# A 2-D convolution block on one NeuronCore: the copy of a rotated half moves from ScalarE to GpSimd

## The chip, the core and the metric

The kernel runs on one NeuronCore of one Trainium2 chip. Five engines work side by side: TensorE (PE, matmuls; its weight loads are PEld), VectorE (DVE), ScalarE (ACT), GpSimd (POOL) and SyncE (SP, which here only issues DMAs). The metric is the device time of one execution in microseconds (us). Before the change it was 19,064.78 us, the median of three runs from 19,036.86 to 19,088.58.

## The reference

The input is x, 4 images of 512 x 512 places with 16 channels, in float32. Two layers follow each other, each with a group normalisation in front and a residual sum behind:

```python
# --- layer 0 (conv_preact) ---
x = x + _L0_conv_ref(_gn(x), L0_conv_h0, L0_conv_numerators, L0_conv_denumerator)
# --- layer 1 (conv_preact) ---
x = x + _L1_conv_ref(_gn(x), L1_conv_kernel, L1_conv_bias, L1_conv_radius)
```

Layer 0 is a convolution by a rational filter, carried out in the frequency domain. Its core is

```python
X = jnp.fft.rfft2(x, s=(2 * l1, 2 * l2), axes=(-3, -2))
Y = jnp.einsum('...hwi,ijhw->...hwj', X, H_full)
y = jnp.fft.irfft2(Y, s=(2 * l1, 2 * l2), axes=(-3, -2))
return y[..., :l1, :l2, :]
```

so at each of the frequencies, 16 input channels are mixed into 16 output channels by a matrix of complex numbers. Layer 1 is a 3 x 3 convolution normalised by the norms of its input and kernel, with an arccosine behind it.

## The kernel before

The program is written in Python with a framework that tracks the tiles, inserts all semaphores, and fills each engine's queue itself: an instruction can stand in its engine's queue earlier than its place in the program, when the framework's own planning finds it ready. Each engine works through its queue in order, so an instruction that waits holds everything behind it.

Four phases run one after the other. `filter_phase` builds the filter, `forward_phase` transforms x along the width, `conv_phase` does the rest of layer 0's convolution, and `last_phase` transforms back and computes layer 1. The change lies in `conv_phase` alone.

`conv_phase` (from L650) works row by row, a row being one frequency along the width. There are 513 of them (L673). The convolution along the height is cut into blocks: for each row there are an overlapped transform of x in 128 frequencies f, 16 input channels with their complex parts on 128 partitions, and a matrix gh of the filter. The tile `xe` of a row (L727) holds 8 "places" of 1,024 numbers a partition:

- place 0 is the transform of the row itself, written by `x_part` (L723) from TensorE's result px;
- places 1 to 3 and 5 to 7 are shifted by 16, 32, ... partitions. They are made through HBM: `x_late` (L738) stores place 0 into `xf_d` with GpSimd's DMA (`store(0, ...)`, L745), multiplies it on GpSimd by a rotation (four multiplies L752, one multiply L753, one add L754, giving the tile `xl`), and stores `xl` too (`store(1, ...)`). `load_xe` (L766) then loads the six places in two DMAs of 1,536 KB (L769), issued by SP;
- place 4 is shifted by 64 partitions: its lower half is the upper half of place 0, its upper half the lower half of `xl`. `half_shift` (L760) copies each half on ScalarE (L763), 64 partitions x 1,024 numbers.

`mix` (L792) multiplies all 8 places by gh into the PSUM tile pm; this is the einsum. `g_part` (L775) makes the next row's gh from g; `over_q` (L812) and `over_g` (L842) take the result back along the height and store it into y_d (L868).

The rows overlap, as written out by hand in `step(n)` (L876): it mixes row n, makes gh of row n + 1, begins x of row n + 2 (`x_part` and `x_late` behind the first quarter, k = 0; `half_shift` behind the third and fourth, k = 2 and 3), and finishes rows n - 1 and n - 2. Loads run ahead: x of row n + 3, g of row n + 2, and the shifted places of row n + 1. Evictions from PSUM (`evict`, L678) go two to ScalarE, one to VectorE in turn. `xl` has one buffer, `xe` three, g and x two each; PSUM has three buffers for pg, two for pm and three shared by px, pz and py.

The queues of a row in the trace, around the change: ACT's is xe (from px), the copy of the plain half, yf, turn, gh, zq, the copy of the rotated half, yf, gh, zq, yo, yf, gh, zq. POOL's is two multiplies L752, the store of place 0, two more, L753, L754, the store of xl, the store of y_d, and the two operations of over_q, zd (L836) and z (L838). SP's is the first xe load, g, the second xe load, x.

Of the kernel before, what the change touches and what calls it, by code (L numbers as in the profile page):

```python
# [46 lines left out]
P = 128  # L47
# [153 lines left out]
def bc(ap, axis, shape):  # L201
    return ap.unsqueeze(axis).to_broadcast(shape)
# [447 lines left out]
def conv_phase(tc, cst, g_d, x_d, y_d):  # L650
    nc = tc.nc
    with ExitStack() as ctx:
# [22 lines left out]
        state = {}  # L675
# [9 lines left out]
        def load_g(n):  # L685
            rc, r, plane = rows[n]
            g = io.tile([P, C, 8 * C], F32, name="g")
            t, w = g.rearrange("p j x -> p (j x)"), C * 8 * C
            if plane is None:
                nc.sync.dma_start(out=t, in_=dram(g_d[rc], r, 0, [w, P], [1, w]))  # L690
            else:
                for to, at in ((0, (0, 96)[plane]), (64, (64, 32)[plane])):
                    nc.sync.dma_start(out=t[to : to + 32], in_=dram(g_d[rc], r, at * w, [w, 32], [1, w]))
                    nc.gpsimd.memset(t[to + 32 : to + 64], 0.0)
            state["g", n] = g

        def load_x(n):
            rc, r, plane = rows[n]
            x = io.tile([P, B, 8 * C], F32, name="x")
            t, w = x.rearrange("p b x -> p (b x)"), B * 8 * C  # L700
            if plane is None:
                nc.sync.dma_start(out=t, in_=dram(x_d[rc], r, 0, [w, P], [1, w]))
            else:
                nc.gpsimd.memset(t[S:], 0.0)
                nc.sync.dma_start(out=t[:S], in_=dram(x_d[rc], r, plane * S * w, [w, S], [1, w]))
            state["x", n] = x

        def turn_x(n):

            for k in range(2) if n == 0 else [n // 64 + 1] if n % 64 == 0 else []:  # L710
                if k < 9:
                    state["own", k] = xlp.tile([P, 2, 64], F32, name="own", bufs=3)
                    nc.sync.dma_start(
                        out=state["own", k].rearrange("p v n -> p (v n)"), in_=cst["own"][:, 128 * k : 128 * k + 128]
                    )
            own, at = state["own", n // 64], slice(n % 64, n % 64 + 1)
            t = xlp.tile([P, 2 * F], F32, name="turn")
            nc.scalar.activation(t, dfs[:, 1], AF.Identity, scale=own[:, 1, at])
            m = xlp.tile([P, 2 * F], F32, name="dfs_n", bufs=2)
            nc.vector.scalar_tensor_tensor(m, dfs[:, 0], own[:, 0, at], t, ALU.mult, ALU.add)  # L720
            state["dfs", n] = m

        def x_part(n, b):  # L723

            if b == 0:

                state["xe", n] = xep.tile([P, 8, F, 2, 2, 2], F32, name="xe")  # L727
            if b % 2 == 0:
                state["px"] = ps_f.tile([P, 2, F, 2], F32, name="px", tag="full")
            px = state["px"]  # L730
            nc.tensor.matmul(px[:, b % 2].rearrange("p f c -> p (f c)"), state["x", n][:, b],
                             state["dfs", n], start=True, stop=True)
            if b % 2:
                evict(state["xe", n][:, 0, :, b // 2], px.rearrange("p k f c -> p f c k"))
            if b == B - 1:
                del state["x", n], state["dfs", n]

        def x_late(n):  # L738

            xe = state["xe", n][:, 0]  # L740
            fl = xe.rearrange("p f h c k -> p f (h c k)")

            def store(half, t):
                at = slice(C, P) if half == 0 else slice(0, P - C)
                nc.gpsimd.dma_start(out=xf_d[n % 4][half * P :, :][at], in_=t[at].rearrange("p f x -> p (f x)"))  # L745

            store(0, fl)
            xl = xlp.tile([P, F, 2, 2, 2], F32, name="xl")
            u = xlp.tile([P, F, 2, 2, 2], F32, name="xu")
            for c in range(2):  # L750
                for h in range(2):
                    nc.gpsimd.tensor_mul(u[:, :, h, c], xe[:, :, h, 1 - c], bc(late[:, 1 + c], 2, [P, F, 2]))  # L752
            nc.gpsimd.tensor_mul(xl.rearrange("p f h c k -> p f (h c k)"), fl, bc(late[:, 0], 2, [P, F, 8]))  # L753
            nc.gpsimd.tensor_add(xl.rearrange("p f h c k -> p (f h c k)"),  # L754
                                 xl.rearrange("p f h c k -> p (f h c k)"),
                                 u.rearrange("p f h c k -> p (f h c k)"))
            store(1, xl.rearrange("p f h c k -> p f (h c k)"))
            state["xl"] = xl

        def half_shift(n, half):  # L760

            dst, src = ((slice(0, 64), state["xe", n][64:, 0]), (slice(64, P), state["xl"][:64]))[half]
            nc.scalar.copy(state["xe", n][dst, 4].rearrange("p f h c k -> p (f h c k)"),  # L763
                           src.rearrange("p f h c k -> p (f h c k)"))

        def load_xe(n):  # L766
            src = xf_d[n % 4]
            for t in (1, 5):
                nc.sync.dma_start(  # L769
                    out=state["xe", n][:, t : t + 3].rearrange("p t f h c k -> p t (f h c k)"),  # L770
                    in_=bass.AP(tensor=src.tensor, offset=src.offset + t * C * XF,
                                ap=[[XF, P], [C * XF, 3], [1, XF]]),
                )

        def g_part(n, j):  # L775


            if j % 4 == 0:
                state["pg"] = [ps_g.tile([P, 4, F], F32, name=f"pg{c}", tag="pg") for c in range(2)]
            g, pg = state["g", n], state["pg"]  # L780
            for c in range(2):
                half = slice(64 * c, 64 * c + 64)
                nc.tensor.matmul(pg[c][:, j % 4], g[half, j], dg[half], start=True, stop=True)  # L783
            if j == 3:
                state["gh", n] = ghp.tile([P, F, 2, C], F32, name="gh")
            if j % 4 == 3:
                for c in range(2):
                    evict(state["gh", n][:, :, c, j - 3 : j + 1], pg[c].rearrange("p j f -> p f j"))
            if j == C - 1:
                del state["g", n]  # L790

        def mix(n, g):  # L792

            if g % 8 == 0:
                state["pm"] = ps_m.tile([P, 8, 8, 2 * B], F32, name="pm")
            xe, gh, pm = state["xe", n], state["gh", n], state["pm"]
            for q in range(4):
                f = g + 32 * q
                nc.tensor.matmul(  # L799
                    pm[32 * q : 32 * q + 32, g % 8], gh[:, f].rearrange("p c j -> p (c j)"),  # L800
                    xe[:, :, f].rearrange("p t h c k -> p t (h c k)"), start=True, stop=True,
                )
            if g == 7:

                state["y", n] = yp.tile([P, 16, 32, 4], F32, name="yf")
            if g % 8 == 7:
                evict(state["y", n][:, :, g - 7 : g + 1].rearrange("p t g x -> p g t x"),
                      pm.rearrange("p g t (h x) -> p g (t h) x", h=2))
            if g == 31:
                del state["xe", n], state["gh", n]  # L810
# [65 lines left out]
        def step(n):  # L876


            def row(k):
                return 0 <= n + k < n_rows  # L880

            if row(3):
                load_x(n + 3)
            if row(2):
                load_g(n + 2)
            if row(1):
                load_xe(n + 1)
            for k in range(4):
                if row(0):
                    for g in range(8):  # L890
                        mix(n, 8 * k + g)
                if row(1):
                    for j in range(4):
                        g_part(n + 1, 4 * k + j)
                if row(-1):
                    for t in range(4):
                        over_q(n - 1, 4 * k + t)
                if row(2) and k == 0:
                    for m in range(B):
                        x_part(n + 2, m)  # L900
                    x_late(n + 2)
                if row(2) and k >= 2:
                    half_shift(n + 2, k - 2)
                if row(3) and k == 2:
                    turn_x(n + 3)
                if row(-2) and k == 2:
                    for m in range(4):
                        over_g(n - 2, m)
# [446 lines left out]
```

## Time and profile before

| what | value |
|---|---|
| the profiled execution, its own time | 19,054.31 us |
| its span in the profile | 19,052.5 us |
| filter phase, about 0 to 5,900 us | 5,900 us |
| forward phase, about 5,900 to 6,950 us | 1,050 us |
| convolution phase, about 6,950 to 16,010 us | 9,060 us |
| last phase, about 16,010 us to the end | 3,042 us |
| busy over the span: PE, DVE, ACT, POOL | 91%, 60%, 51%, 61% |

The phases overlap a little at their borders. Durations of the convolution phase's instructions around the change, from its groups of instructions (out<-in, partitions x elements, count | busy us, mean ns):

```profile
L752 POOL TENSOR_TENSOR xu<-xe,c_late 128x256 f32<-128x256 f32 x2036 | 1382.8, 705 | 848.5 <-ACT xe L683 824.5 <-DVE xe L681 15.6
L754 POOL TENSOR_TENSOR xl<-xl,xu 128x1024 f32<-128x1024 f32 x509 | 1200.3, 2358 | 39.9
L753 POOL TENSOR_TENSOR xl<-xe,c_late 128x1024 f32<-128x1024 f32 x509 | 1006.5, 1977 | 0.0
L763 ACT COPY xe<-xl 64x1024 f32<-64x1024 f32 x509 | 534.6, 1050 | 1861.8 <-POOL xl L754 1861.8
L763 ACT COPY xe<-xe 64x1024 f32<-64x1024 f32 x509 | 532.1, 1045 | 685.4 <-DVE xe L681 685.4
```

The last column is the time that the engine stood idle just before the group, and what ended most of it. A row takes one of each of the last four, and four of the first. In this phase the DMAs of a row carry 3,072 KB of shifted places, 1,024 KB of g, 256 KB of x, two stores of 448 KB and one of 256 KB.

### The profile page before, as it was taken

To read this page: it belongs to the slowest core of one execution; us is meant where nothing else is said; L and a number is where in the kernel's file an instruction comes from. 1 tells how busy PE (TensorE), PEld (TensorE's weight loads), DVE (VectorE), ACT (ScalarE), POOL (GpSimd) and SP (SyncE) were. 2 spreads that over 40 slices of the span, in tenths; PEclk is the share of its full clock that TensorE was granted. 3 is DMA by queue.
4 is the path that set the end of the run, shared out by engine and by line. 5 is a ranking of instruction groups with operands and counts; after the bars stand their busy time and mean duration, and the time that the engine had idled before them with its cause. 6 is when DMAs were issued, how large, how long until landed. Compare 5 with 4: busy or idle time off the path is not lost. (4 is left out here: it accounts for less than half of the span.)

```text
span 19052.5 us, 536690 instructions
## 1 busy us (share of the span) xinstructions
PE 17293.1 (91%) x227020; PEld 12605.2 (66%) x227020; DVE 11398.8 (60%) x23961; ACT 9747.4 (51%) x17871; POOL 11564.3 (61%) x12445
## 2 busy tenths in 40 slices
PE   8899999999999988898888888888888888979999
PEld 5455555555554457777777777777777776868888
DVE  8877777777763335555555555555555554347656
ACT  4455555555552235555555555555555553107777
POOL 7577777777771126666666666666666664127655
PEclk7899999999999999999999999999999999999999
DMA  3755455555557668888888888888888887796321
GB/s 100 206 153 148 137 150 150 146 139 149 149 151 223 187 211 320 323 322 324 320 322 317 322 327 317 322 324 323 320 325 323 321 320 282 268 321 210 131 72 62
DMA packets 2918658, 4543.39 MB, mean 238 GB/s; under 512 B 117442, under 2 KB 2086300, under 8 KB 2809374
## 3 DMA queue, kind: packets, MB, share of 16 engines
q1 hardware_dynamic: 2686062, 3768.91, 58.5%
q0 software_dynamic: 174896, 605.89, 8.3%
q10 hardware_dynamic: 55296, 134.24, 2.1%
q8 instruction: 1789, 29.31, 0.6%
q14 instruction: 615, 5.04, 0.1%
HBM read 3031.23 MB, written 1477.31 MB: 237 GB/s over the span
## 5 line engine op out<-in xcount | busy, mean ns | idle before, releaser
L783 PE MATMUL pg<-c_dg,g 64*128 64x128 f32 x32832 | 2842.9, 291 | 320.9 <-ACT gh L683 159.5
L799 PE MATMUL pm<-xe,gh 128*32 128x64 f32 x131328 | 2403.4, 222 | 576.2 <-issue 353.1
L799 PEld LDWEIGHTS pm<-xe,gh 128*32 128x32 f32 x131328 | 2012.8, 110 | 1180.2 <-issue 996.4
L783 PEld LDWEIGHTS pg<-c_dg,g 64*128 64x128 f32 x32832 | 2283.2, 190 | 662.7 <-issue 262.5
L372 PE MATMUL pg<-c_dinv,sp 128*128 128x256 f32 x8192 | 2278.4, 426 | 294.3 <-ACT st L377 193.8
L828 DVE TENSOR_TENSOR z<-zq,pz 128x256 f32<-128x256 f32 x2052 | 862.0, 420 | 2617.2 <-ACT zq L827 2534.6
L348 DVE RECIPROCAL dn<-dn 128x256 f32<-128x256 f32 x1024 | 1790.8, 1749 | 778.3 <-POOL dn L341 778.0
L372 PEld LDWEIGHTS pg<-c_dinv,sp 128*128 128x128 f32 x8192 | 1609.9, 207 | 946.8 <-ACT st L377 215.3
L681 DVE COPY gh<-pg 128x512 f32<-128x512 f32 x2046 | 1410.5, 689 | 1294.1 <-PE pg L783 1289.6
L417 PE MATMUL pt<-ev_in,c_todd 128*128 128x512 f32 x4096 | 1970.1, 606 | 45.6 <-DMA ev_in<-g_d 27.0
L752 POOL TENSOR_TENSOR xu<-xe,c_late 128x256 f32<-128x256 f32 x2052 | 1393.4, 705 | 856.3 <-ACT xe L683 832.3
L335 ACT COPY ab<-pab 128x512 f32<-128x512 f32 x2048 | 1104.2, 592 | 1130.1 <-POOL m L355 333.3
L683 ACT COPY yf<-pm 128x512 f32<-128x512 f32 x2046 | 1210.5, 592 | 919.0 <-PE pm L799 904.3
L377 ACT COPY st<-pg 128x256 f32<-128x256 f32 x2048 | 1072.6, 623 | 1024.0 <-PE pg L372 619.3
L763 ACT COPY xe<-xl 64x1024 f32<-64x1024 f32 x513 | 538.8, 1050 | 1877.0 <-POOL xl L754 1877.0
L350 POOL TENSOR_TENSOR x<-ab,ab 128x256 f32<-128x256 f32 x1024 | 875.8, 855 | 933.6 <-ACT ab L335 907.0
L1208 PE MATMUL pc<-l_band,xn 128*128 128x160 f32 (+3 forms) x9024 | 1374.8, 309 | 65.0 <-DVE e_o L1255 64.0
L683 ACT COPY gh<-pg 128x512 f32<-128x512 f32 x2058 | 1201.2, 584 | 402.0 <-PE pg L783 393.6
L820 PE MATMUL pz<-c_ident,yf 128*128 128x128 f32 x8208 | 1378.2, 291 | 27.2 <-issue 25.4
L1208 PEld LDWEIGHTS pc<-l_band,xn 128*128 128x128 f32 x9024 | 1218.8, 197 | 224.7 <-issue 147.2
L329 PEld LDWEIGHTS pab<-c_e,u 18*128 18x128 f32 x8192 | 723.5, 188 | 809.5 <-ACT st L377 452.5
L417 PEld LDWEIGHTS pt<-ev_in,c_todd 128*128 128x128 f32 x4096 | 806.8, 198 | 669.9 <-issue 514.6
(195 smaller groups left out, 33846.4 us busy)
## 6 DMA issues: line engine op xcount, KB each, us to landing
xe<-xf_d SPq DMA_DIRECT2D x1026, 1536.0 KB, 10.3
g<-g_d SPq DMA_DIRECT2D x511, 1024.0 KB, 9.9
g_d<-st SPq DMA_DIRECT2D x64, 4096.0 KB, 34.3
ev_in<-g_d SPq DMA_DIRECT2D x1024, 256.0 KB, 4.8
g_d<-ot SPq DMA_DIRECT2D x1024, 256.0 KB, 2.9
xf_d<-xe POOLq DMA_DIRECT2D x513, 448.0 KB, 8.3
xf_d<-xl POOLq DMA_DIRECT2D x513, 448.0 KB, 5.3
x_d<-xo SPq DMA_DIRECT2D x128, 1024.0 KB, 5.1
```

The lines of the kernel that those rows point to most:

```text
L335: nc.scalar.copy(w["ab"][n], pp[n])
L348: nc.vector.reciprocal(w["dn"], w["dn"])
L372: nc.tensor.matmul(pg[:, k].rearrange("p a x -> p (a x)"), w["sp"][:, k, c, :], dinv[:, 2 * kp + k, c, :], start=(c == 0), stop=(c == 1),)
L377: nc.scalar.copy(st[a][:, :, i].rearrange("p (q k x) -> p k q x", q=2, k=4)[:, 2 * kp : 2 * kp + 2], pg[:, :, a].rearrange("p k (q x) -> p ...
L417: nc.tensor.matmul(pt, todd[:, c, kc, hh * P : hh * P + P], ev[:, kc, c], start=(kc == 0), stop=(kc == 1),)
L681: nc.vector.tensor_copy(dst, src)
L683: nc.scalar.copy(dst, src)
L752: nc.gpsimd.tensor_mul(u[:, :, h, c], xe[:, :, h, 1 - c], bc(late[:, 1 + c], 2, [P, F, 2]))
L783: nc.tensor.matmul(pg[c][:, j % 4], g[half, j], dg[half], start=True, stop=True)
L799: nc.tensor.matmul(pm[32 * q : 32 * q + 32, g % 8], gh[:, f].rearrange("p c j -> p (c j)"), xe[:, :, f].rearrange("p t h c k -> p t (h c k ...
L820: nc.tensor.transpose(pz[:, t % 4].rearrange("p v q x -> p (v q x)"), y[:, at].rearrange("p g x -> p (g x)"), ident)
L1208: nc.tensor.matmul(pc[:, lo:hi, :].rearrange("p w j -> p (w j)"), xns[q][:, h * P + dh : h * P + dh + P], bands[dh][:, o : o + hi - lo, :] ...
```

## The change

The two halves of place 4 are copied where `x_late` ends, and `half_shift` with its call in `step` goes. The plain half stays on ScalarE; the rotated half is copied by GpSimd, behind the store of `xl` in the program. What is copied, and to where, is the same.

```diff
             store(1, xl.rearrange("p f h c k -> p f (h c k)"))
-            state["xl"] = xl
-
-        def half_shift(n, half):
-
-            dst, src = ((slice(0, 64), state["xe", n][64:, 0]), (slice(64, P), state["xl"][:64]))[half]
-            nc.scalar.copy(state["xe", n][dst, 4].rearrange("p f h c k -> p (f h c k)"),
-                           src.rearrange("p f h c k -> p (f h c k)"))
+
+            nc.scalar.copy(state["xe", n][:64, 4].rearrange("p f h c k -> p (f h c k)"),
+                           xe[64:].rearrange("p f h c k -> p (f h c k)"))
+            nc.gpsimd.tensor_copy(state["xe", n][64:, 4].rearrange("p f h c k -> p (f h c k)"),
+                                  xl[:64].rearrange("p f h c k -> p (f h c k)"))
...
                     x_late(n + 2)
-                if row(2) and k >= 2:
-                    half_shift(n + 2, k - 2)
                 if row(3) and k == 2:
                     turn_x(n + 3)
```

## The prediction

> **What bounds the kernel now.** I read the page's slices first. Between about 6,950 and 16,010 us the machine does 513 times the same thing, one "row" of the convolution, and the change touches nothing else; so I asked for the busy time of that stretch, then for the waits in it.
>
> ```profile
> core 0: us, PE busy (x) PEld busy (x) DVE busy (x) ACT busy (x) POOL busy (x), PEclk, DMA share, GB/s
> 6950.00:16010.00 9060.00, 8096.70 (x183886) 6452.52 (x183888) 4913.59 (x13257) 4772.90 (x8688) 5764.49 (x5631) 0.98 0.87 321
> ```
>
> 9,060 us over 513 rows is 17.66 us a row. POOL works 11.2 us of it, ACT 9.3, DVE 9.6, TensorE 15.8; the DMA engines are busy 87% of it, 15.4 us. TensorE's figure holds overlap: the shortest start-to-start times of its 15 groups of matmuls in a row add up to 14.8 us. So two things are near the row time, and none fills it: somebody waits. Two views of waits (waiter <- releaser: us in total, times, longest), ACT's and SP's, show two candidates:
>
> ```profile
> ACT xe L763 <- POOL xl L754: 1861.8, 509, 6.5
> ```
> ```profile
> SPq L769 <- DMA xf_d<-xl: 6509.3, 508, 15.0
> ```
>
> The first is the wait that the change removes: ACT stands 3.7 us in every row in front of the copy of the rotated half, because GpSimd has not finished L754. The second is 12.8 us a row: SP waits for the store of xl to land before it may load the rotated copies of that row (L769). What each does is seen in the timeline of one row, whose x_part begins at 10,755.42. First ACT and TensorE:
>
> ```profile
> 10760.87 0.38 ACT L827 COPY zq<-pz 128x256 f32<-128x256 f32 x1
> 10764.98 1.05 ACT L763 COPY xe<-xl 64x1024 f32<-64x1024 f32 x1 [3.74 <-POOL xl L754]
> 10766.05 0.59 ACT L683 COPY yf<-pm 128x512 f32<-128x512 f32 x1
> ```
> ```profile
> 10767.18 1.16 PE L783 MATMUL pg<-c_dg,g 64*128 64x128 f32 x14 [1.00 <-ACT gh L683]
> ...
> 10770.81 1.10 PE L799 MATMUL pm<-xe,gh 128*32 128x64 f32 x64 [1.48 <-DMA xe<-xf_d]
> ```
>
> ACT is held from 10,761.2 to 10,766.0; seven evictions queue behind it until 10,769.4, and TensorE loses about 1 us for PSUM. That forms a loop of one row: x_part, GpSimd's rotation, the held copy, the backlog, the next x_part. Undisturbed rows repeat at exactly 16.9 us, and that is this loop. But the average row is 17.66, and in the row shown TensorE, after its loss, still waits 1.48 us for a load. The other loop is in SP's timeline (start, us, instruction; the first load of each row):
>
> ```profile
> 10702.13 0.37 SPq L769 DMA_DIRECT2D xe<-xf_d  x1
> ...
> 10719.41 0.37 SPq L769 DMA_DIRECT2D xe<-xf_d  x1
> ...
> 10737.10 0.37 SPq L769 DMA_DIRECT2D xe<-xf_d  x1
> ...
> 10754.51 0.37 SPq L769 DMA_DIRECT2D xe<-xf_d  x1
> ...
> 10772.19 0.37 SPq L769 DMA_DIRECT2D xe<-xf_d  x1
> ...
> 10789.42 0.37 SPq L769 DMA_DIRECT2D xe<-xf_d  x1
> ```
>
> The steps are 17.3, 17.7, 17.4, 17.7, 17.2. Inside one step (windows; the last two columns are DMA share and GB/s):
>
> ```profile
> 10737.10:10738.10 1.00, 1.00 (x15) 0.88 (x16) 0.34 (x2) 0.52 (x1) 0.92 (x2) 1.00 0.06 16
> 10738.10:10745.10 7.00, 7.00 (x176) 6.00 (x176) 4.46 (x11) 4.33 (x8) 5.43 (x7) 1.00 0.97 349
> 10745.10:10752.10 7.00, 5.90 (x109) 4.26 (x106) 2.86 (x10) 3.97 (x8) 4.01 (x4) 1.00 1.01 395
> 10752.10:10753.10 1.00, 0.60 (x23) 0.44 (x27) 0.96 (x4) 0.36 (x1) 0.00 (x0) 1.00 0.93 356
> 10753.10:10754.50 1.40, 1.40 (x69) 1.31 (x59) 1.05 (x4) 0.52 (x1) 1.29 (x2) 1.00 0.19 75
> ```
>
> About 15 us of full DMA engines, then 1.4 us until the store's landing is known, then 1 us until the next burst's first packets. All loads of a row (xe, g, xe, x, 4.3 MB) stand behind that landing in SP's queue. I paired each first load with the next one and with the store of xl issued between them (GpSimd's timeline), over 500 rows. When the store is issued 10.5 to 11 us after the load, the next load follows 17.53 us after the first (median); 11 to 11.5: 17.51; 11.5 to 12: 17.49; 12 to 12.5: 17.49; 12.5 to 13: 17.52; 13 to 13.5: 17.60; 13.5 to 14: 17.71; 14 to 14.5: 17.93. So **the DMA loop takes 17.5 us whenever the store comes early enough**, and moving the store by 2.5 us changes nothing: its packets wait behind the burst. Only a store later than 13 us costs time. The mean over all rows is 17.69, so lateness costs 0.15 to 0.2 us a row and the DMA loop the rest.
>
> **What the Trainium skill says.** DMA: Bandwidth & Descriptors, "Issuing engines are not separate DMA queues": DMAs of all issuers share the same 16 engines. The trace agrees: GpSimd's stores start about 3.7 us after issue under SP's burst and 0.6 us after it when the engines are free. The same page, "Anatomy of one DMA", puts most of a DMA's fixed cost on the write receipt; here 1.4 us lie between the end of the packets and the next load's issue. GPSIMD Engine Reference, "Instruction dispatch": a Pool instruction that reads partitions which another core wrote in the one before needs a wait on its completion. The trace has such waits already (0.29 us between L754 and its store).
>
> **The change, part by part.**
> 1. ACT loses the copy of the rotated half, 1.05 us, and the wait in front of it, 3.7 us. Its backlog, seven evictions of some 3.3 us, moves ahead to where TensorE's results come, so the 16.9 us loop is gone. What is late next: on TensorE's side 14.8 us plus its hiccups; on the DMA's, 17.5.
> 2. ACT's copy of the plain half is written earlier in the program. In the trace it already runs there, directly behind the eviction of xe (it waits 1.35 us for DVE's half of it), so: 0.
> 3. GpSimd gains a copy of 64x1024 f32. No row shows GpSimd copying as much, or writing other partitions than it reads. From below: its memset of 32x2048 took 1.798 us, 0.88 ns an element, so 0.90 us, and about 0.1 more, as its copy of 128x4 took 0.195: 1.0 us. The skill's GPSIMD Engine Reference, section 3.1, gives 1.03 cycles an element for such bodies at 1.2 GHz, an estimate of 0.88 us. From above: the multiply of 128x1024, 1.977 us with two inputs. I take 1.1.
> 4. What stands behind it on POOL: the store of y_d (L868), 12.8 us after x_part's start today because it waits for ACT's held eviction; then zd and z, which wait for DVE. The copy runs from 10.4 to 11.5 us after that start; the eviction for y_d should by then be done, so y_d goes at 11.5, earlier than today. zd can't start before about 13.3 (over_q of the last quarter, then ACT and DVE), z ends near 16, and the next row's first multiply starts at 17.5 + 1.7 = 19.2. So the copy is covered by some 1.2 + 3.3 us of idle POOL; without cover it would cost its 1.1 us.
> 5. The store of xl is issued ahead of the copy, 9.8 us after x_part's start, as before. Does a compute instruction behind a GpSimd DMA delay its packets? In the filter stage k_apad's load is followed by a TENSOR_TENSOR after 0.01 us, and its first packet comes 0.64 us after the issue, as with idle behind it: 0. A delay of up to 2.4 us would be swallowed by the flat part of the DMA loop anyway.
> 6. SP's loads: same order, same wait.
>
> **The sum.** With ACT's hold gone, TensorE reaches each row's first mix before its loads have landed. The second xe load lands 15.6 us after the first one's issue, mix starts 0.14 later, x_part 2.6 after that, the store 9.8 after that: 28.15 us after the issue, or 28.15 - 17.5 = 10.65 after the next row's. This lies in the flat part, with 2.4 us to spare for hiccups, which TensorE also makes good at 2.5 us a row instead of 0.6. The 58 rows whose mix started within 0.2 us of the landing had a DMA loop of 17.48 us already today. I take 17.52: (17.67 - 17.52) x 513 = 77 us. The profiled run took 19,054.31 us (span 19,052.5), so 18,977; the median of the three runs is 10 us higher, and on its scale I say **18,985 us**, 0.4% less. Most of the removed stall turns into TensorE waiting for the xe loads.
>
> **The rivals.**
> - *ACT's hold is the real limit* (chance 0.08). For it: the 1,862 us and the exact 16.9. Then the slack between landing and mix, about 2 us a row, would leave the two-row path of load, mix, rotation, store with today's mean store time: (15.6 + 0.1 + 12.4 + 5.4) / 2 = 16.75 us a row, 470 us less: 18,595. Against it: the flat 17.5.
> - *Nothing to be measured* (0.24): the excess over 17.5 comes from the DMA side itself, from late landings that TensorE's speed doesn't mend, or earlier work on other engines gives it back. 19,040 to 19,065.
> - *The copy is slow on GpSimd* (0.18, slower). Place: POOL's queue ahead of y_d, zd and z, and by them the next row's rotation. POOL has 11.2 us of work a row and 0.6 of dependent gaps, so it becomes the bound from 17.5 - 11.8 = 5.7 us for the copy, five times my price; the crossing of partitions, unseen so far, is what could do it. At 6.5 us the row takes 18.3: (18.3 - 17.67) x 513 = 320 more, 19,385.
>
> **How the numbers follow.** My forecast has 0.50. About 0.3%, 57 us, is what can be told from no change; my 77 lie little above, so of the 0.50 I give 0.08 to "within" and of the 0.24 some 0.02 to slower and 0.02 to faster. Faster: 0.42 + 0.08 + 0.02 = 0.52; within: 0.08 + 0.20 = 0.28; slower: 0.18 + 0.02 = 0.20. The forecast's own range is 18,940 to 19,030. For 8 in 10 it reaches over the "nothing" case and into the slow one: 18,890 to 19,115; the first rival and most of the last stay outside.
>
> **What would show it.** Right: ACT's wait on POOL xl gone; TensorE's waits for ACT's gh and zq gone, and its mix waiting on the xe load in nearly every row; SP's first loads at 17.5 us steps; the GpSimd copy near 1.1 us; y_d issued earlier. Wrong: steps well under 17.5, a copy of several us, the store of xl moved away from 9.8 us behind x_part, or a queue filled in another order.

## The result: no change, and the profile after

| | before | after |
|---|---|---|
| median of 11 runs each, on one chip | 19,057.6 us | 19,061.82 us |
| range of the runs | 19,034.59 to 19,088.58 | 19,046.10 to 19,094.12 |
| the profiled execution, its own time | 19,054.31 us | 19,049.05 us |

The ratio of after to before is 1.0005, with an interval of 0.9995 to 1.0014. The 77 us that the prediction forecast are not there: the rival "nothing to be measured" came true. The 19,062 us lie outside the forecast's own range (18,940 to 19,030), and inside the one for 8 in 10 (18,890 to 19,115) only because that one was stretched over this rival.

The same views as before the change, of the kernel after. First the waits of ACT in the convolution phase (waiter <- releaser: us in total, times, longest):

```profile
ACT yf L683 <- PE pm L797: 1655.1, 1265, 8.0
...
ACT xe L759 <- DVE xe L681: 662.2, 509, 3.8
```

The wait of 1,861.8 us for xl is gone. ACT now waits for TensorE: L797 is the matmul of mix. The groups of instructions on GpSimd show the copy that came in and the store of y_d behind it:

```profile
L761 POOL COPY xe<-xl 64x1024 f32<-64x1024 f32 x508 | 526.1, 1036 | 23.5
L866 POOL DMA_DIRECT2D y_d<-yo x506 | 294.6, 582 | 298.9 <-ACT yo L683 280.0 <-DVE z L826 11.9 <-issue 1.9
```

The copy takes 1.036 us, and the store waits 280 us for ACT's eviction, where it waited 1,304 before. All that is as it was meant. But the wait of SP for the store of xl, in SP's waits, is what it was (6,509.3 us before), and SP's timeline of five rows (the first load of each) still steps by 17.5, 18.2, 17.5 and 17.4 us:

```profile
SPq L767 <- DMA xf_d<-xl: 6532.5, 508, 15.0
```
```profile
9060.47 0.37 SPq L767 DMA_DIRECT2D xe<-xf_d  x1
...
9077.97 0.37 SPq L767 DMA_DIRECT2D xe<-xf_d  x1
...
9096.20 0.37 SPq L767 DMA_DIRECT2D xe<-xf_d  x1
...
9113.74 0.37 SPq L767 DMA_DIRECT2D xe<-xf_d  x1
...
9131.17 0.37 SPq L767 DMA_DIRECT2D xe<-xf_d  x1
```

TensorE's waits tell what took the place of ACT's hold ("issue" is idle time for which the trace names no releaser). Before:

```profile
PE pg L783 <- ACT gh L683: 147.9, 174, 2.9
PE pm L799 <- DMA xe<-xf_d: 73.7, 51, 3.0
```

and after:

```profile
PE pm L797 <- issue: 382.6, 362, 3.7
PE pm L797 <- DMA xe<-xf_d: 279.8, 139, 5.3
PE pg L781 <- issue: 157.2, 114, 3.1
```

The wait for ACT's eviction of gh has dropped out, and mix now waits 3.8 times as long for the loads of xe. Last, the whole stretch of the convolution in one line (busy us of PE, PEld, DVE, ACT, POOL; clock; DMA share; GB/s):

```profile
6950.00:16010.00 9060.00, 8084.73 (x184001) 6471.79 (x184002) 4980.28 (x13265) 4379.92 (x8171) 6274.29 (x6140) 0.96 0.87 321
```

ACT's 4,773 us became 4,380 and POOL's 5,764 became 6,274; the DMA share stayed at 0.87. TensorE's granted clock went from 0.98 to 0.96. That small column turned out to matter.

**Where the time went, piece by piece.** From a row's first load the way leads to its mix, from there to the x_part that stands behind that mix in TensorE's queue, which belongs to the row after next, to the store of that row, and to the first load of that row. So the first four pieces of the table go round in two rows, and their sum is twice the last line. They are means over the same 505 rows of each trace:

| piece | before | after |
|---|---|---|
| first load issued to the start of mix, one row later | 17.36 us | 17.10 us |
| mix to x_part | 2.75 | 2.98 |
| x_part to the store of xl | 9.87 | 9.90 |
| store to the next first load | 5.40 | 5.43 |
| load to load (the mean row) | 17.69 | 17.70 |

The first line is where the forecast gain should have shown: the prediction put it at 15.74 us (15.6 + 0.14), with mix at the landing of the loads in nearly every row. It fell by 0.26 us. Of the 253 rows for which the trace tells the landing, mix started within 0.2 us of it in 99, against 58 before. The second line takes 0.23 of the 0.26 back. Between mix and x_part TensorE stands idle for 0.06 us a row (0.02 before), so most of this is not a wait: it is the clock. The record of the granted clock shows pieces of 3.41 us (or a multiple of it) at half speed. Counting half of their time as lost, they cost 0.10 us a row before and 0.28 after between mix and x_part; over the whole row 0.35 and 0.61. One such row of the changed kernel, TensorE's timeline, and then the windows around it (the column with 1.00 and 0.50 is the clock):

```profile
9077.50 1.16 PE L781 MATMUL pg<-c_dg,g 64*128 64x128 f32 x14
9078.59 0.66 PE L818 MATMUL pz<-c_ident,yf 128*128 128x128 f32 x4
9079.09 1.89 PE L731 MATMUL px<-dfs_n,x 128*128 128x256 f32 x8
...
9090.94 0.48 PE L781 MATMUL pg<-c_dg,g 64*128 64x128 f32 x2
9094.25 1.10 PE L797 MATMUL pm<-xe,gh 128*32 128x64 f32 x64 [2.82 <-DMA xe<-xf_d]
9095.28 1.98 PE L781 MATMUL pg<-c_dg,g 64*128 64x128 f32 x14
9097.19 1.12 PE L818 MATMUL pz<-c_ident,yf 128*128 128x128 f32 x4
9098.10 2.25 PE L731 MATMUL px<-dfs_n,x 128*128 128x256 f32 x8
```
```profile
9091.00:9094.20 3.20, 0.42 (x3) 0.23 (x2) 1.63 (x6) 0.45 (x2) 2.17 (x3) 1.00 0.96 380
9094.20:9095.40 1.20, 1.16 (x66) 1.09 (x68) 0.00 (x0) 0.00 (x0) 0.47 (x1) 1.00 0.18 72
9095.40:9098.80 3.40, 3.40 (x20) 3.09 (x21) 0.69 (x1) 1.54 (x3) 0.00 (x0) 0.50 0.44 149
9098.80:9102.00 3.20, 3.20 (x83) 2.65 (x84) 2.91 (x7) 1.42 (x2) 1.77 (x3) 1.00 1.05 415
```

TensorE waits 2.82 us for the load, starts mix, and 1.2 us later runs at half clock for 3.4 us: the 14 matmuls of g_part take 1.98 us where the row above took 1.16, the transposes 1.12 for 0.66, px 2.25 for 1.89. So a wait in front of mix is paid a second time, right on the way to x_part and the store. A half-clock piece began in an idle time of TensorE, or within 2 us behind it, in 2% (before) and 4% (after) of the cases when it was 0.8 to 1.6 us long, in 55% and 54% when it was 1.6 to 2.2 us, and in 80% and 75% when it was 2.2 to 3.0 us. The change gathered TensorE's scattered waits into fewer and longer ones: idle times over 1.6 us went from 139 to 217, and those right in front of a row's first mix from 32 to 100, while all its idle time together, over 0.15 us each, hardly moved (945 and 968 us in the phase).

### The profile page after: what moved, and what is told of

Same layout as the page of the kernel before. It is cut to its first block, busy times and chain, and to the rows that moved or that the text cites. A ratio compares the mean times of both kernels' runs of the same rounds, so it can differ in the third digit from the quotient of the medians.

```text
span 19047.3 us, 537201 instructions
## 1 busy us (share of the span) xinstructions
PE 17279.6 (91%) x227020; PEld 12631.8 (66%) x227020; DVE 11466.3 (60%) x23961; ACT 9357.8 (49%) x17358; POOL 12079.5 (63%) x12958
## 5 line engine op out<-in xcount | busy, mean ns | idle before, releaser
L797 PE MATMUL pm<-xe,gh 128*32 128x64 f32 x131328 | 2439.4, 224 | 726.8 <-issue 389.6
L781 PE MATMUL pg<-c_dg,g 64*128 64x128 f32 x32832 | 2778.4, 294 | 171.7 <-issue 157.2
L797 PEld LDWEIGHTS pm<-xe,gh 128*32 128x32 f32 x131328 | 2039.6, 112 | 1326.3 <-issue 1227.7
L834 POOL TENSOR_TENSOR zd<-z 128x512 f32<-128x512 f32 x513 | 649.3, 1266 | 1066.1 <-DVE z L826 1059.8
```

The costliest lines, as they stand in the source:

```text
L797: nc.tensor.matmul(pm[32 * q : 32 * q + 32, g % 8], gh[:, f].rearrange("p c j -> p (c j)"), xe[:, :, f].rearrange("p t h c k -> p t (h c k ...
```

## The experiments

Two theories at the start. *The DMA loop*: load, mix, x_part, store sets the row, ACT's hold had been hidden, and clock and late stores take back what little there was. *The copy on GpSimd*, or the queue behind it, costs what ACT saves. Later a third question: what TensorE itself needs for a row. All ratios are to the kernel before, run beside. "g by ACT" means that the load of g is issued by ACT, so that it no longer stands between the two loads of xe in SP's queue.

| run | time, us | ratio to before, interval |
|---|---|---|
| e1 before, hold twice | 19,809.22 | 1.0382 (1.0365 to 1.0399) |
| e2 after, copy four times | 19,159.95 | 1.0044 (1.0029 to 1.0059) |
| e3 before, g by ACT | 19,077.72 | 0.9997 (0.9988 to 1.0005) |
| e4 after, g by ACT | 19,028.13 | 0.9969 (0.9956 to 0.9982) |
| e5 before, g loaded once | 18,897.01 | 0.9921 (0.9898 to 0.9944) |
| e6 after, g loaded once | 18,554.00 | 0.9731 (0.9715 to 0.9747) |
| e7 after, mix last | 18,902.91 | 0.9912 (0.9897 to 0.9926) |
| e8 after, mix last, g by ACT | 19,120.91 | 1.0031 (1.0021 to 1.0041) |
| e9 before, mix last | 18,924.14 | 0.9922 (0.9909 to 0.9934) |
| e10 after, fill | 19,771.49 | 1.0367 (1.0353 to 1.0381) |
| e11 before, fill | 19,865.55 | 1.0414 (1.0399 to 1.0428) |

**e1: make ACT's hold longer.** In the kernel before, the rotated half is copied twice:

```diff
-            nc.scalar.copy(state["xe", n][dst, 4].rearrange("p f h c k -> p (f h c k)"),
-                           src.rearrange("p f h c k -> p (f h c k)"))
+            for _ in range(1 + half):
+                nc.scalar.copy(state["xe", n][dst, 4].rearrange("p f h c k -> p (f h c k)"),
+                               src.rearrange("p f h c k -> p (f h c k)"))
```

> The kernel before, with the rotated half copied twice on ACT (the second copy writes the same values again). DMA loop theory (a row takes 17.5 us because the loads wait for the store of xl; ACT's hold forms a shorter loop of 16.9 us beside it): ACT's loop grows by 1.05 to 17.95 us and passes the DMA loop, so a row takes 18.0 to 18.2, 150 to 270 us more in all. Theory that ACT's hold counts in full: 1.05 x 513 = 540 us more. Theory that ACT's hold costs TensorE nothing: no change.

Measured: about 750 us more, beyond every forecast. The quickest rows lie at 18.06 to 18.1 us, which is 16.9 + 1.05 + 0.1, so the ACT loop is there as described. But the mean row is 19.23. In front of a row's first mix TensorE now stands idle for 1.6 us (median; 0.4 before), above all for ACT, whose evictions are late behind the two copies (the trace names the last of them, zq). It loses 1.10 us a row to the half clock (0.35 before). The wait and the stretch:

```profile
PE pm L800 <- ACT zq L828: 601.3, 371, 2.1
```
```profile
7000.00:15500.00 8500.00, 7192.33 (x159079) 5748.16 (x159083) 4263.09 (x11483) 4577.48 (x7948) 4958.24 (x4859) 0.94 0.80 296
```

The clock fell to 0.94. Stalls without a releaser on TensorE grew too, by 179 us in all, and the store came later against the load (14.8 us behind it, 12.2 before), where the loop is longer. What each of them is worth alone was not tried. What follows: here a regular gap in front of mix cost more than the 540 us that were put in.

**e2: make the GpSimd copy longer.** In the changed kernel the copy is done four times:

```diff
-            nc.gpsimd.tensor_copy(state["xe", n][64:, 4].rearrange("p f h c k -> p (f h c k)"),
-                                  xl[:64].rearrange("p f h c k -> p (f h c k)"))
+            for _ in range(4):
+                nc.gpsimd.tensor_copy(state["xe", n][64:, 4].rearrange("p f h c k -> p (f h c k)"),
+                                      xl[:64].rearrange("p f h c k -> p (f h c k)"))
```

> The kernel after, with GpSimd's copy done four times over, 3.1 us more of GpSimd a row. DMA loop theory: GpSimd then has 15.3 us of work and 0.6 of gaps in 17.5, and zd and z still end ahead of the next row's rotation: within 0.3% of the kernel after. Theory that the copy on GpSimd gave the gain back: three times its 1.04 us is lost again in each row, up to 1,600 us more.

Measured: 3.1 us more on GpSimd in each row, 1,594 us over 513 rows, cost some 75 us (19,159.95 beside 19,084.03 of the kernel before, which the changed kernel equals). So one copy of 1.036 us can hardly have taken back the gain. The store of y_d went out 14.7 us after x_part's start (11.45 in the changed kernel); the loop at the same store time was up to 0.5 us longer. That y_d's packets then run into the next burst is likely, but only argued.

**e3 and e4: shorten the DMA loop by the queue.**

```diff
-                nc.sync.dma_start(out=t, in_=dram(g_d[rc], r, 0, [w, P], [1, w]))
+                nc.scalar.dma_start(out=t, in_=dram(g_d[rc], r, 0, [w, P], [1, w]))
```

> The kernel before, with the g load issued by ACT instead of SP, so that it doesn't wait for the store of xl and doesn't stand ahead of the second xe load. DMA loop theory: the DMA loop gets shorter by up to the 2.4 us in which the engines stood idle, and ACT's loop of 16.9 us is what is left: a row of 16.9 to 17.2, 250 to 400 us less. Theory that TensorE's own row with its stalls for instructions is the bound: no change within 0.3%.

> The kernel after, with the g load issued by ACT instead of SP. DMA loop theory: without ACT's hold the row follows the shorter DMA loop below 16.9, to 16.2 to 16.6 us, 550 to 750 us less than the kernel before, and some 300 less than the kernel before with the same edit. TensorE theory: no change. Theory that ACT's hold never mattered: the same as the kernel before with the same edit.

Both missed: 0 instead of 250 to 400, and 0.3% instead of 550 to 750 us. e4 is 50 us quicker than e3, where some 300 were forecast; their intervals lie apart. The loop itself did shorten where the store comes early: with the store 11 to 12 us after the load it is 16.8 (e3) and 16.9 us (e4) where it was 17.5. With the store 13 to 14 us after it, it is 17.5 where it was 17.6. The wait of mix for xe has all but gone (7 us in e4). TensorE's waits of e4:

```profile
PE pm L797 <- issue: 653.8, 593, 4.0
PE pg L781 <- issue: 191.1, 158, 3.7
PE py L855 <- issue: 36.9, 43, 1.8
```

In its place stands "issue": all of it together, over 0.15 us each, went from 570 us (before) to 909 (e3) and 923 (e4). That is some 0.7 us a row more, as much as the loop had given where the store is early. What these stalls are is told in the last section.

**e5 and e6: shorten the DMA loop by its bytes.** The g of row 2 is kept for all later rows:

```diff
         def load_g(n):
+            if n > 2:
+                state["g", n] = state["g", 2]
+                return
...
-            if j == C - 1:
+            if j == C - 1 and n != 2:
                 del state["g", n]
```

> The kernel before, with the matrix g of row 2 kept and used for all later rows, so that 1,024 KB of loads a row are left out (the filter of the other rows is not read; output differs). DMA loop theory: the burst gets 2.6 us shorter, the DMA loop falls to about 15 us, and ACT's loop of 16.9 us is left as the bound: rows of 16.9 to 17.0, 340 to 400 us less. Theory that TensorE's stalls for instructions are the bound whatever the loops are: less too, as they grow with the load on the DMA engines, but then not with a median of just 16.9.

> The kernel after, with the same loads left out. DMA loop theory: without ACT's hold nothing stands at 16.9, and the row falls to TensorE's own 14.8 us and its stalls for instructions, 15.6 to 16.2: 750 to 1,050 us less than the kernel before, and 400 or more less than e5. Theory that ACT's hold never cost anything: the same as e5. Theory that GpSimd's copy gave the gain back: e6 not faster than e5.

This settled the first question. Waits of ACT in e5 (up to 15,500 us), and TensorE's in e6:

```profile
ACT xe L766 <- POOL xl L757: 1710.5, 490, 6.5
```
```profile
PE pm L800 <- issue: 426.2, 366, 4.5
PE pg L784 <- issue: 129.6, 99, 3.4
...
PE pm L800 <- DMA xe<-xf_d: 12.4, 10, 3.7
```

In e5 seven rows of ten lie between 16.87 and 17.06 us: ACT's loop of 16.9, as the prediction had read it. In e6 that loop is gone and the rows go down to 14.9. With fewer bytes to load the change is worth 343 us (18,897.01 to 18,554.00); with the loads as they are, nothing. Both sizes missed: 167 us instead of 340 to 400 in e5, and 510 instead of at least 750 in e6, which is 343 below e5 and not 400. They point the same way: in e6 all of TensorE's waits with a releaser come to 27 us in the phase, and with neither ACT's hold nor the loads in its way it still needs 16.68 us a row (97 of 505 rows with a store later than 14 us among them), not some 15.

**e7, e8 and e9: take mix's wait off the way to the store.** In `step`, the eight mixes of a quarter move from its front to its end, so that x_part does not stand behind the wait for xe:

```diff
             for k in range(4):
-                if row(0):
-                    for g in range(8):
-                        mix(n, 8 * k + g)
                 if row(1):
...
+                if row(0):
+                    for g in range(8):
+                        mix(n, 8 * k + g)
```

> The kernel after, with mix at the end of each quarter of a row's program instead of at its start, so that TensorE has g_part, over_q and x_part to do while the xe loads are on their way. Theory that the gain was given back by TensorE's wait for these loads and the slower clock behind it: the clock's loss falls from 0.60 to below 0.4 us a row, the wait in front of mix to near nothing, the store of xl is issued earlier, and the row takes 17.3 to 17.5, 100 to 200 us less. Theory that only the DMA burst counts, whenever the store comes: a row of 17.5 to 17.6, within 0.5% of the kernel after.

> e7 with the g load issued by ACT as in e4. If the loop of loads and store and TensorE's stalls for instructions share the blame: the loop no longer binds, TensorE's 14.8 and 1.7 us of stalls are left: 16.6 to 17.0, 350 to 550 us less. If the stalls grow again with the load on the DMA engines, as from the kernel after to e4: no more than e4's gain.

> The kernel before, with the same move of mix to the end of each quarter as in e7; ACT keeps the rotated copy. Beside e7 (18,903) it tells what the change itself is worth once TensorE no longer stands in front of mix for the loads. If GpSimd's rotation still holds ACT for 3 to 4 us a row, TensorE feels it (its loads are no longer what it waits for): 18,980 to 19,060, some 80 to 150 us slower than e7, and ACT's wait on xl above 1,500 us. If the change is worth nothing in this order either: within 40 us of e7.

e7 is 0.9% faster than the kernel before, 161 us against its runs beside it (as expected), and so faster than the changed kernel too. Its store of xl is issued 10.4 us after the first load (median; 12.2 in both kernels), where the loop takes some 17.5, as before. But it takes 17.07 us where the store comes at 9 to 10 and 16.65 at 8 to 9, so the flat 17.5 is no floor. The wait for xe has nearly gone (279.8 us in the changed kernel):

```profile
PE pm L797 <- DMA xe<-xf_d: 14.3, 16, 2.3
```

The expected fall of the clock loss below 0.4 us a row was missed: 0.47, and the stalls without a releaser grew to 988 us. The clock gives 0.14 of the 0.31 us by which e7's row is shorter than the changed kernel's; in e9 its loss rose (0.53, after 0.35 in the kernel before), and the row still fell, from 17.69 to 17.46 us. So the gain came mainly by the order. e8 was 0.3% slower than the kernel before, where 350 to 550 us less were forecast: the framework filled TensorE's queue in another order, with x_part and mix cut in parts and mixed, so it says nothing on the theories. e9 lies within the interval of e7, 0.9922 beside 0.9912. Waits of ACT in e9:

```profile
ACT xe L763 <- POOL xl L754: 2123.6, 510, 6.5
```

ACT is held as long as ever, 2,124 us, and it costs nothing, against my expectation of 80 to 150 us: TensorE waits 14 us for ACT's gh in the whole phase. So in this order too the change is worth nothing.

**e10 and e11: fill the gap in front of mix.**

```diff
-                nc.tensor.matmul(pg[c][:, j % 4], g[half, j], dg[half], start=True, stop=True)
+                for _ in range(7 if j == C - 1 else 1):
+                    nc.tensor.matmul(pg[c][:, j % 4], g[half, j], dg[half], start=True, stop=True)
```

> The changed kernel, with the last pair of g_part's matmuls of a row issued seven times instead of once: 12 matmuls more, about 0.083 us each, 1.0 us of TensorE work a row, right ahead of the wait for the xe loads. Clock theory (gaps of over 1.6 us in front of mix halve the clock behind them): such gaps fall from 217 to under 120 and the time lost to the half clock from 0.61 us a row to under 0.45, so that the 1.0 us costs much less than itself: 0 to 250 us more in all, row 17.7 to 18.1. TensorE as the bound: the full 1.0 us, 500 us more. If the clock has nothing to do with the gaps, its loss stays near 0.6.

> The kernel before with the same 12 matmuls more. Its gaps in front of mix are shorter and it loses only 0.35 us a row to the half clock, so less is won back: by the clock theory it pays more for the 1.0 us than e10 does, 100 to 350 us more, and the changed kernel is then the faster of the two by 50 us or more. If both pay alike, the clock isn't what took the gain back.

The size of the fill was wrong, and so was the forecast of the times: TensorE's timeline of e10 shows the group with the fill beside one without it,

```profile
10006.42 1.18 PE L782 MATMUL pg<-c_dg,g 64*128 64x128 f32 x16
...
10011.56 3.72 PE L782 MATMUL pg<-c_dg,g 64*128 64x128 f32 x40
```

so the 12 matmuls (24 records) took 2.56 us from start to start, not 1.0. For that the row grew by 1.37 us in e10 (19.07) and by 1.56 in e11 (19.25). The rest, 1.2 us, had been waiting time. Idle times over 1.6 us fell from 217 to 82 in e10 and from 139 to 71 in e11, and the clock loss with them, from 0.61 to 0.30 us a row and from 0.35 to 0.20. This is the half of the test that held: more work on TensorE, less half clock. With the loads no longer awaited, the kernel with the change is the faster of the two, 19,771 to 19,866, some 94 us; but ACT's hold, which is in e11 alone, does that too (118.9 us of waits for gh in e11's view, none in e10's), so it says nothing for the clock. In e10 TensorE waits for next to nothing but "issue":

```profile
PE pm L798 <- issue: 290.6, 303, 3.7
PE pg L782 <- issue: 130.6, 121, 2.9
PE py L856 <- issue: 39.8, 39, 2.5
```

That gives TensorE's own row a second time: 19.07 - 2.56 = 16.51 us.

## Where the prediction was right and where wrong, step by step

1. *ACT loses 1.05 us of copy and 3.7 of waiting; the 16.9 us loop goes.* Right: the wait is gone, e5 shows the loop alone and e6 its absence.
2. *The plain half costs nothing.* Right as far as shown: it runs behind the eviction of xe, waiting 662 us for DVE's half (685 before).
3. *The copy on GpSimd takes 1.1 us.* 1.036; the rival of a slow copy fell with it. The Trainium skill's GPSIMD Engine Reference, section 3.1, from which I had the estimate of 0.88 us for the body, fits a copy that changes partitions as well.
4. *The queue behind it is covered, y_d goes out at 11.5 us.* 11.45, and e2 shows that three more such copies cost only some 75 us together.
5. *The store of xl stays where it is.* 9.90 us after x_part's start, 9.87 before.
6. *SP's loads keep order and wait.* Right.

**The step that failed is the sum**, and in it two sentences: that TensorE "reaches each row's first mix before its loads have landed", and that it makes hiccups good "at 2.5 us a row instead of 0.6". The 2.5 was 17.5 less some 15, and the 15 was the sum of the shortest start-to-start times of TensorE's groups, 14.8. That is a shortest row (e6's quickest take 14.9), not a mean one. Where TensorE waits for almost nothing that has a releaser (5 us over e10's phase, 27 over e6's), its mean row is 16.5 (e10) and 16.7 us (e6): to the 14.8 come in e10 about 1.0 us of stalls for which no releaser is seen (528 us over the phase), 0.3 us of half clock, and 0.4 that I can't place. In these two runs the DMA engines were the less busy, with a share of 0.81 and 0.77. Where they were as busy as in the changed kernel (0.87) or a little more (0.88), TensorE's mean row was longer still, though it waited for hardly more with a releaser: 17.59 us in e4, 17.39 in e7 and 17.46 in e9 (32, 68 and 31 us of such waits), with stalls of 1.8 to 2.0 us a row. That is the length of the DMA loop itself. So a late row is made good at 1.0 us a row at most, and with the loads as they are at next to nothing; ACT's loop had left 0.6. The stalls and the half clock both stood in the profile of before, as "issue" in TensorE's waits and as the 0.98 of the clock; I took them for hiccups that are made good, when they are a part of the mean row.

Hence the second term failed: the store was to come 10.65 us after the first load in nearly every row. Its median stayed at 12.2, and late stores did not get fewer: 14 us or later in 37 of 505 rows before and 43 after. The flat part of the loop was read rightly for the store times that the two kernels have (after: 17.49 at 10 to 11 us, 17.58, 17.51, 17.60 in the next three), and so was what lies outside it (18.30 at 14, 19.09 at 15); the rows simply didn't move into it. But "17.5 us whenever the store comes early enough" is too wide: e7 has 17.07 and 16.65 us with the store at 9 to 10 and 8 to 9. The third term was missing: the change makes fewer and longer waits of many short ones, and behind them the clock halves, on the way from mix to the store. This piece took back 0.23 of the 0.26 us that the first one had won, 0.18 of it by the clock. The numbers of the pieces are means of one execution each.

The case is neither "the DMA loop alone" nor "TensorE alone". The DMA loop takes 17.5 us with the store where these kernels have it; TensorE with its stalls needs 16.5 to 16.7 us where the DMA engines are less busy, and 17.4 to 17.6 where they are as busy as here. What lies over 17.5 is rows in which TensorE made the store late. To remove ACT's hold, which had kept TensorE near 16.9, could gain little while the loads stay as they are: nothing in the order of the kernel and in that of e7 and e9, 50 us from e3 to e4, 343 us where a quarter of the loaded bytes is left out (e5 to e6).

## What to carry to other kernels

Before a forecast lets an engine "make good" its hiccups, take its row from a mean in which nothing is waited for, stalls and clock included, and not from the sum of its shortest times: here 16.5 to 16.7 us, and 17.4 to 17.6 under the full load of DMAs, stood against 14.8, and the whole forecast lay in between. Here two loops of nearly the same length shared an engine, and relieving the shorter one moved its wait to the other; look instead for what stands in the longer loop without need, as mix in front of x_part did here (0.8 to 0.9%, with the change or without it). And several short waits gathered into one cost more here than they did apart, as the one was long enough to lower the clock.

## What the runs showed of the hardware that I had not expected

**The half clock comes after short gaps, and goes with the idle time within one piece.** The Trainium skill, TensorE: Matmul & The Clock Gate, "Why this matters for your kernels", asks for no gaps of TensorE above about 3 us. Here shorter ones were enough. In the thirteen traces (before, after, e1 to e11) a half-clock piece began in a gap of 1.6 to 2.2 us, or within 2 us behind it, in 19 to 56% of the cases, with one of 2.2 to 3.0 us in 60 to 83%, and with one of 0.8 to 1.2 us in at most 2% (11% in e1, where gaps follow each other closely). Where a gap lies explains much of the difference. In each trace all half-clock pieces of the convolution phase begin on one grid of 3.413 us, to within 0.003 us. Cut along that grid, with TensorE's idle time added up in each piece, the thirteen phases show: behind a piece with more than 2.0 us idle the next one ran at half clock in 845 of 845 cases, behind 1.6 to 1.8 us in 279 of 534, behind less than 1.4 us in 258 of 31,424. So a gap of 2 us within one piece is paid a second time, and one that falls across two pieces mostly isn't. This is a coincidence counted over many gaps; that the half clock goes down when gaps are filled is shown by e10 and e11, and that it goes up when they are forced by e1.

**TensorE's stalls without a releaser are instruction fetches, by all signs.** In the convolution phase of the kernel before, every idle time of TensorE over 0.3 us for which the trace names no releaser, 481 of them with 559 us in all, ends 1.1 to 1.7 us after the end of a packet of the instruction queue (q8); after, all 479. A random moment has a median distance of 3.1 us. The queue's line in the DMA view of the convolution phase, before:

```profile
q8 instruction: 1440, 23.59, 1.0%
```

1,440 packets, 16 KB each, 2.8 a row. The Trainium skill's Runtime: NRT & Kernel Launch, "Instruction fetch mechanics", describes such a refill through a DMA queue of the engine's own in blocks of 16 KiB, and calls its cost mostly hidden; here it seems to cost TensorE 1.1 us a row. No run changed the fetches alone, so this rests on the timing. The stalls came to 915 to 1,001 us over the phase in e3, e4, e7 and e9, all four with TensorE hardly waiting for loads and a DMA share of 0.87 to 0.88, and to 472 to 603 in e5, e6, e10 and e11, with a share of 0.74 to 0.81. That a wait had merely covered them can't be the whole of it, as TensorE waits for hardly anything else in e4 and e9 (32 and 31 us) and in e6 and e10 (27 and 5 us) alike. Nor did the packets of the queue take longer: 0.95 to 0.96 us (median) in every run. It is mainly more of them that hold TensorE up, 704 and 728 stalls over 0.3 us in e3 and e4 beside 481 in the kernel before, 467 in e6 and 433 in e10. That busier DMA engines delay the start of a fetch would fit, but e1 (751 us at a share of 0.80) and e8 (718 at 0.88) don't lie on that line, and the cause stays open.
